# A graph layer on one core: 56 instead of 52 tiles fetched row by row, other waits for SyncE's transfers, and x gathered for 8 instead of 10 quads

## The chip, the cores and the metric

The kernel runs on one core of one Trainium2 chip. The metric is the device time of one execution in microseconds; the time before is the median of three runs. Engines are named as in the profile: PE (TensorE), PEld (its weight loads), DVE (VectorE), ACT (ScalarE), POOL (GpSimd) and SP (SyncE, which only issues transfers). A "q" behind an engine's name (ACTq, SPq) marks what its sequencer issues.

## The reference

A message-passing layer over 206,250 edges and 6,250 nodes of 128 features (8 heads of 16), with the edges sorted by receiver, followed by a residual and a normalization:

```python
w_ij = silu(edge_feats @ rad_W1 + rad_b1) @ rad_W2 + rad_b2
w_ij = w_ij + silu(chi_scalar @ sph_W1 + sph_b1) @ sph_W2 + sph_b2      # per edge, 128 wide
q_i = (x @ Wq)[receivers];  k_j = (x @ Wk)[senders];  v_j = (x @ Wv)[senders]
alpha = (q_i * w_ij * k_j).sum over each head / sqrt(16) * cutoffs
out = segment_sum(alpha * v_j, receivers) / 16
return layernorm(x + out)
```

## The kernel before, in words

**Tiles, quads, groups.** Edges are cut into tiles of 128; four tiles are a quad (512 edges), four quads a group. There are 403 quads in 101 groups. `order` is the order in which quads are worked on; the loop over `g` and `slot` handles one quad a slot, at place `i = 4 g + slot` of `order`.

**The start.** K and V of all nodes are computed in 13 chunks and stored to a table in device memory, `kv_tab` (L353), one row of 1 KB per node. Edges need the rows of their senders. The table isn't ready at once, so for the first `XQ` quads POOL gathers rows of x instead (`gather_x`, L134 writing `msg`), and PE projects them to K and V as it does the chunks. `AHEAD` is 14: the quads `order[XQ:14]` are gathered from `kv_tab` before the loop starts. Beside the start's quads PE transposes the receivers' relative places (`turn_rel`), which are stored as `rel_lin` and read back broadcast as `relb`, one transfer a group.

**Two ways to fetch rows.** The usual way is an indirect DMA of POOL (`gather`, L134), one per tile: 128 rows of `kv_tab`, so four a quad. For `ROW_TILES` quads, spread evenly over the places 20 to 392, the last tile is fetched otherwise: by 128 single transfers of one row (L191, into `wide`), 64 issued by SP and 64 by ACT, with the rows' addresses loaded into registers 32 at a time (L186). `load_rows(i)` runs at the end of every slot and issues the share of the tile that is due, so that the whole tile is on its way 8 places ahead of its quad. A quad with such a tile needs three gathers of POOL.

**A slot.** PE does sums of older messages (L614), the first layers of quad `i + 2` (L516, into `ph`), the receivers' q of quad `i + 1` (L525, into `pq`) and the second layers (L563, into `pw`). ACT applies the two activations of a quad (L546, `silus`), with copies of small products between them (`copies`), and later issues its row transfers. DVE multiplies `pq` by K (L575), by `pw` (L583), reduces over heads (L585), scales (L589) and forms messages with V (L602). POOL gathers for quad `i + 14`, each of the four gathers behind one of the last four `pw` products of an older quad (`old[-QT:]`).

**SP's transfers in the loop.** One each a group: x (L281), feats (L218), relb (L229) and the finished rows (`out`, L731). SP works its queue in order. x and feats carry a wait for a product of PE (`past`), so all that stands behind them in the queue waits too. Group sums are normalized four groups at a time; their rows are written by `write_rows(1, i)`.

Of the kernel before, what the change touches and what calls it, by code (L numbers as in the profile page):

```python
# [21 lines left out]
SP = mybir.EngineType.SP  # L22
ACT = mybir.EngineType.Activation
WAIT = mybir.DependencyInfo(mybir.DependencyClass.Sync, mybir.DependencyReason.DATA)

P = 128
# [9 lines left out]
NG = math.ceil(E / (P * GT))  # L36
NT = NG * GT
# [6 lines left out]
W = 32  # L44
LB = 4
ROW_BYTES = 2 * D * 4
XQ = 10
RING = 16
ROW_TILES = 52
ROW_FIRST = 20  # L50
ROW_LAST = 392
ROW_LEAD = 8
ROW_UNIT = 32
ROW_ACT = 64
XU = 4
WRITE_LAG = 3
READY_LAG = 2
# [3 lines left out]
XL = 3  # L61
# [6 lines left out]
def gnn_kernel(ctx, tc, x, src, dst, weight, edges, rad_W1, rad_b1, rad_W2, rad_b2,  # L68
# [38 lines left out]
    row = const.tile([P, 1], F32, name="row")  # L107
# [22 lines left out]
    def quad_of(name, bufs, width=D):  # L130
        return ep.tile([P, QT, width], F32, name=name, bufs=bufs)
# [11 lines left out]
    row_of = {}  # L143
    row_done = {}
    rows_left = {SP: [], ACT: []}
    row_sems = [tc.alloc_semaphore(f"rows_{n}") for n in range(ROW_SEMS)]
    row_count = [0] * ROW_SEMS

    def next_rows(engine, n):

        left = rows_left[engine]
        while n > 0 and left:
            row = next(left[0], None)
            if row is None:
                left.pop(0)
                continue
            row()
            n -= 1

    r_of = {}  # L160
    feats_of, relb_of, act_of, kv_of, hot_of, hotT_of, x_of, q_of, msg_of = ({} for _ in range(9))
# [11 lines left out]
    def load_rows(i):  # L173

        k = next((k for k in range(ROW_TILES) if i <= row_at[k] - ROW_LEAD), None)
        start = None if k is None else (row_at[k - 1] if k else ROW_FIRST) - ROW_LEAD + 1
        if k is None or i < start:
            return
        q = order[row_at[k]]
        slots = row_at[k] - ROW_LEAD + 1 - start  # L180
        table = kv_tab.bitcast(U8).rearrange("(o n) b -> o (n b)", o=1)

        def rows_by(engine, name, a, b):
            for e in range(a, b, ROW_UNIT):
                m = min(ROW_UNIT, b - e)
                rows = nc.values_load_multi_w_load_instructions(  # L186
                    at_i[k:k + 1, e:e + m], engines=(name,), min_val=0,
                    max_val=(N - 1) * ROW_BYTES,
                    skip_runtime_bounds_check_because="senders are nodes")[1]
                for p, r in zip(range(e, e + m), rows):  # L190
                    yield lambda p=p, r=r: signalled(engine.dma_start(  # L191
                        row_of[q][p:p + 1, 0, :].bitcast(U8), table[:, ds(r, ROW_BYTES)]))

        def signalled(o):
            tc.no_tile_sem_insts.add(o.ins.name)
            tc.add_to_no_dep_group(f"rows_{q}", o.ins)
            o.then_inc(row_sems[k % ROW_SEMS], 16)
            row_count[k % ROW_SEMS] += 16
            row_done[q] = row_sems[k % ROW_SEMS], row_count[k % ROW_SEMS]

        n = P - ROW_ACT
        if i == start:
            row_of[q] = quad_of("wide", 3, P)[:, :2, :].rearrange("p t d -> p (t d)")[:, None, :]
            rows_left[SP].append(rows_by(nc.sync, SP, 0, n))
            rows_left[ACT].append(rows_by(nc.scalar, ACT, n, P))
        for engine, m in ((SP, n), (ACT, ROW_ACT)):
            a, b = (math.ceil(m * j / slots) for j in (i - start, i - start + 1))
            next_rows(engine, b - a)

    def kv_parts(q, t):  # L210

# [4 lines left out]
    def load_feats(g, mark=None):  # L216
        feats_of[g] = gp.tile([P, EG // 2], F32, name="feats", bufs=3)
        o = nc.sync.dma_start(feats_of[g], edges[g])  # L218
        if mark is not None:
            tc.add_manual_dep(o.ins, mark.ins.name, WAIT, reason="one signal of TensorE a quad")  # L220
# [51 lines left out]
    def load_x(g, mark=None):  # L272

        if g not in r_of:
            n = min(XU, NG - g)
            rows = nc.values_load_multi_w_load_instructions(
                gb_i[:1, g:g + n], engines=(SP,), min_val=0, max_val=(N - P) * D * 4,
                skip_runtime_bounds_check_because="the table is clamped to it")[1]
            r_of.update(zip(range(g, g + n), rows))
        x_of[g] = gp.tile([P, D], F32, name="x", bufs=XL + 4)  # L280
        o = nc.sync.dma_start(x_of[g].bitcast(U8), rows_from(x, r_of[g]))  # L281
        if mark is not None:
            tc.add_manual_dep(o.ins, mark.ins.name, WAIT, reason="one signal of TensorE a quad")
# [21 lines left out]
    with tc.tile_pool(name="nodes", bufs=1) as nodes, \  # L305
# [21 lines left out]
                nc.sync.dma_start(xs[:N - (c + full) * P, full, :], x[(c + full) * P:, :])  # L327

        def gather_x(q):
            xs_of[q, "x"] = xs = quad_of("msg", XQ)  # L330
            for t in range(QT):
                gather(xs[:, t, :], x, src_x[:, q * QT + t:q * QT + t + 1])

# [100 lines left out]
        def turn_rel(t):  # L434

            n = min(P, NT - t)
            pt = nps.tile([P, QT, P], F32, name="pt", bufs=3)
            nc.tensor.transpose(pt[:n, 0, :], rel[:, t:t + n], ident)
            nc.scalar.activation(relT[:n, t // P, :], pt[:n, 0, :], AF.Copy)
# [38 lines left out]
        for i, (k, n) in enumerate(work):  # L478
            if i + 2 < len(work):
                turn(*work[i + 2])  # L480
            kvs = k_and_v(k, n)
            for o, w in smalls[i:i + 1]:
                nc.scalar.dma_start(o, w)
            if i >= len(chunks):
                kv_of[k[0]] = kvs
                a = (i - len(chunks)) * 5 // 4
                for t in range(a * P + P, min(((i - len(chunks) + 1) * 5 // 4 + 1) * P, NT), P):
                    turn_rel(t)
                for f in beside.get(i, []):
                    f()  # L490
                continue
            store(k, kvs)
            if k + 8 < len(chunks):
                load_nodes(k + 8)
            if k == 4:
                nc.sync.dma_start(src_i, src)
            for f in beside.get(k, []):
                f()
            if i == len(chunks) - 1:
                load_rel(0, gp, 1)  # L500
                load_feats(0)
                nc.sync.dma_start(scale, weight)
        for q in order[XQ:AHEAD]:
            gathers(q)
# [5 lines left out]
    with tc.tile_pool(name="ps", bufs=1, space=PSUM) as pp, tc.tile_pool(name="loop", bufs=1) as lp:  # L510
# [85 lines left out]
        def messages(q, alpha, t=slice(0, QT), marks=()):  # L596

            if t.start == 0:
                msg_of[q] = quad_of("msg", XQ)
            for u, kv in kv_parts(q, t):  # L600
                n = u.stop - u.start
                o = nc.vector.tensor_tensor(  # L602
                    msg_of[q][:, u, :].rearrange("p t (h e) -> p t h e", e=HD),
                    kv[:, :, D:].rearrange("p t (h e) -> p t h e", e=HD),
                    alpha[:, u.start - t.start:u.stop - t.start, :, None].to_broadcast(
                        [P, n, HEADS, HD]), op=OP.mult)
                behind(o, marks, 3)
# [39 lines left out]
        def part_sums(g):  # L647
            n = quads_in(g) * W
            part_of[g] = gp.tile([P, D], F32, name="part")
            nc.scalar.activation(part_of[g][:n, :], po_of[g][:n, :], AF.Copy)  # L650
# [103 lines left out]
            nc.vector.tensor_scalar(general, found, 0.0, None, op0=OP.is_gt)  # L754

        written, ready, ready_at = [], [], []
        load_feats(1)
        load_rel(1, lp, 4)
        load_feats(2)
        load_rel(2, lp, 4)  # L760
        for g in range(1, XL):
            load_x(g)
        silus(order[0], first_layers(order[0]))
        pick(1)
        q_at_edges(order[0])
# [1 line left out]
        multiply(order[0])  # L767
        marks = weigh(order[0])
        mark = marks[-1]
        for g in range(NG - 1):  # L770
            for slot, j in enumerate((0, 2, 1, 3)):
                q = g * NQ + j
                i = g * NQ + slot
                turned, past, old = None, mark, marks
                if slot == 0 and g == CHECK + len(checks) + 1:
                    verdict()
                if slot == 0:
# [7 lines left out]
                        mark = sum_quads(g - 1, t)  # L785
                first_layers(order[i + 2])
                mark = q_at_edges(order[i + 1])
                marks = weigh(order[i + 1])

                def copies():  # L790
                    if turned:
                        turned()
                    if 1 <= g and slot == 3:
                        part_sums(g - 1)

                silus(order[i + 2], mark, marks, copies)
                if ready and ready_at[-1] <= i:
# [5 lines left out]
                if slot == 0:  # L803
                    if g + XL < NG:
                        load_x(g + XL, past)
                if slot == 2:
                    if g + 3 < NG:
                        load_feats(g + 3, past)
                if slot == 3 and g + 3 < NG:
                    load_rel(g + 3, lp, 4)  # L810
                if slot == 0 and 1 <= g:
                    one_hots(g)
# [3 lines left out]
                        pick(g + 2)  # L816
                if slot == 2 and 1 <= g:
                    place(g - 1)
                write_rows(1, i)
                if slot == (3 if g < NG - 2 else 2):  # L820
                    if 2 <= g:
                        statistics(g - 2)
# [224 lines left out]
```

## Time and profile before

| what | value |
|---|---|
| median of three runs | 1974.61 us (1973.51 to 1975.46) |
| profiled execution | 1977.56 us |
| its span, first to last instruction | 1975.8 us |
| mean granted TensorE clock | 0.941 |
| PE, DVE, POOL, ACT busy | 90%, 77%, 75%, 33% |
| gathers of POOL | 40 of x, 1520 of kv |
| row transfers of SP, ACT | 3328 each |

A row of the timeline reads: start, duration, engine, line, operation, what is written and read, number of instructions merged, and in brackets the engine's idle time before it with what ended it. A row of a group ends with total and mean duration, then idle time before. Issuing a transfer does not count as busy time of ACT or SP.

### The profile page before, as it was taken

How to read it: one execution, taken by the hardware profiler on the slowest of the kernel's cores; microseconds unless marked ns; L12 is line 12 of the kernel's file. 1: busy time of each engine (PE TensorE's matmuls, PEld its weight loads, DVE VectorE, ACT ScalarE, POOL GpSimd, SP SyncE). 2: the span in 40 equal slices, each digit the busy share in tenths (PEclk: the TensorE clock that was granted, in tenths of full speed). 3: DMA queues.
4: the chain of work that ended last, by engine and by line, in shares of the span. 5: the costliest groups of instructions: out<-in, count | busy, mean ns of one | idle time of the engine just before them, and what ended most of it. 6: DMA issues, size and time to landing. Idle time of an engine off the chain costs nothing. (4 is left out here: it accounts for less than half of the span.)

```text
span 1975.8 us, 57697 instructions
## 1 busy us (share of the span) xinstructions
PE 1781.9 (90%) x16014; PEld 1482.9 (75%) x16014; DVE 1520.3 (77%) x3403; ACT 642.5 (33%) x1362; POOL 1481.0 (75%) x1570
## 2 busy tenths in 40 slices
PE   9799999999998999998989889988988888888998
PEld 8687778777777777777877777777767777777776
DVE  6688788888877777777777777776877877777778
ACT  3233333333233333332323332323323333232334
POOL 7777777777777777777777777777777777777775
PEclk9899999999989989899989999899999999898989
DMA  9455555555555555555555555555545455555543
GB/s 318 144 153 155 158 154 157 149 148 151 159 155 156 149 159 152 147 155 145 157 144 156 155 147 154 149 150 149 157 142 158 143 156 155 145 154 147 155 142 94
DMA packets 152293, 304.92 MB, mean 154 GB/s; under 512 B 39852, under 2 KB 86300, under 8 KB 151964
## 3 DMA queue, kind: packets, MB, share of 16 engines
q0 software_dynamic: 74240, 201.95, 36.4%
q1 hardware_dynamic: 69568, 95.42, 15.1%
q10 hardware_dynamic: 8156, 3.82, 0.9%
q8 instruction: 127, 2.08, 0.4%
q14 instruction: 202, 1.65, 0.3%
HBM read 287.58 MB, written 13.46 MB: 152 GB/s over the span
## 5 line engine op out<-in xcount | busy, mean ns | idle before, releaser
L134 POOL DMA_INDIRECT kv<-kv_tab,src_i x1520 | 1440.9, 948 | 469.1 <-PE pw L563 174.0
L546 ACT ACTIVATE act<-ph,b 128x512 f32<-128x512 f32 x806 | 554.8, 689 | 1275.2 <-PE pq L525 767.4
L563 PE MATMUL pw<-w,act 128*128 128x128 f32 x6448 | 883.1, 294 | 0.0
L563 PEld LDWEIGHTS pw<-w,act 128*128 128x128 f32 x6448 | 803.6, 203 | 96.7 <-issue 79.8
L516 PE MATMUL ph<-feats,w 32*128 32x512 f32 x1612 | 521.8, 670 | 38.3 <-ACT act L546 35.7
L525 PE MATMUL pq<-q,hotT 32*128 32x128 f32 x3224 | 489.3, 293 | 19.1 <-DVE kq L575 18.8
L575 DVE TENSOR_TENSOR kq<-pq,kv 128x512 f32<-128x512 f32 (+1 forms) x403 | 270.6, 671 | 285.4 <-DMA kv<-kv_tab,src_i 123.5
L525 PEld LDWEIGHTS pq<-q,hotT 32*128 32x128 f32 x3224 | 409.9, 195 | 49.8 <-DVE kq L575 47.9
L585 DVE TENSOR_REDUCE side<-kq 128x32 f32<-128x512 f32 x403 | 279.8, 694 | 42.7 <-PE pw L563 1.3
L602 DVE TENSOR_TENSOR msg<-kv,side 128x512 f32<-128x512 f32 (+1 forms) x404 | 270.3, 669 | 44.2 <-DVE side L589 2.4
L583 DVE TENSOR_TENSOR kq<-pw,kq 128x512 f32<-128x512 f32 x403 | 274.0, 680 | 0.0
L516 PEld LDWEIGHTS ph<-feats,w 32*128 32x128 f32 x1612 | 143.3, 190 | 144.4 <-ACT act L546 74.1
L558 PE MATMUL pw<-brow,onesb 3*128 3x512 bf16 x403 | 158.9, 394 | 0.6 <-DVE kq L583 0.6
L614 PE MATMUL po<-msg,hot 128*32 128x128 f32 x3200 | 156.8, 294 | 0.0
L655 PE MATMUL pq<-part,to 128*128 128x128 f32 x200 | 48.7, 328 | 88.8 <-DVE kq L575 88.5
L589 DVE TENSOR_TENSOR side<-side,scale 128x32 f32<-128x32 f32 x400 | 79.8, 200 | 42.6 <-DVE side L585 0.9
L655 PEld LDWEIGHTS pq<-part,to 128*128 128x128 f32 x200 | 32.9, 207 | 100.3 <-DVE kq L575 86.7
L614 PEld LDWEIGHTS po<-msg,hot 128*32 128x32 f32 x3200 | 72.3, 112 | 38.9 <-issue 5.6
L258 DVE TENSOR_TENSOR hotT<-relb,side 128x512 f32<-128x512 bf16 x101 | 68.7, 680 | 0.0
L252 PE MATMUL pq<-wq,xT 128*128 128x128 f32 x200 | 44.3, 305 | 26.5 <-DVE kq L575 26.1
L263 DVE TENSOR_TENSOR hot<-rel,side 128x512 f32<-128x512 f32 x100 | 68.0, 680 | 0.0
L252 PEld LDWEIGHTS pq<-wq,xT 128*128 128x128 f32 x200 | 32.4, 203 | 32.1 <-DVE kq L575 31.4
(121 smaller groups left out, 843.7 us busy)
## 6 DMA issues: line engine op xcount, KB each, us to landing
wide<-kv_tab SPq DMA_DIRECT2D x3328, 1.0 KB
wide<-kv_tab ACTq DMA_DIRECT2D x3328, 1.0 KB
feats<-in_edges SPq DMA_DIRECT2D x101, 512.0 KB
kv<-kv_tab,src_i POOLq DMA_INDIRECT x1520
relb<-rel_lin SPq DMA_DIRECT2D x101, 128.0 KB
x<-in_x SPq DMA_DIRECT2D x101, 64.0 KB
out<-y SPq DMA_DIRECT2D x101, 64.0 KB
kv_tab<-kv SPq DMA_DIRECT2D x12, 512.0 KB
```

The source lines that it names most:

```text
L134: return nc.gpsimd.indirect_dma_start(out=o, out_offset=None, in_=table, in_offset=bass.IndirectOffsetOnAxis(ap=index, axis=0))
L516: return nc.tensor.matmul(act_of[q, i], w1[r0:r0 + R, :], feats_of[g][r0:r0 + R, c0:c0 + EQ], start=True, stop=True)
L525: o = nc.tensor.matmul(pq_of[q][:, t, :], hotT_of[g][b, t * P:(t + 1) * P], q_of[g][b, :], start=True, stop=True)
L546: o = nc.scalar.activation(act, act_of[q, i], AF.Silu, bias=b1[:, i:i + 1])
L558: nc.tensor.matmul(pw, onesb, brow.rearrange("p t d -> p (t d)"), start=True, stop=False)
L563: o = nc.tensor.matmul(pw[:, t, :], act_of[q, i][:, t * P:(t + 1) * P], w2[:, i, :], start=False, stop=(t == QT - 1 and i == 1))
L575: o = nc.vector.tensor_tensor(kq_of[q][:, u, :], pq_of[q][:, u, :], kv[:, :, :D], op=OP.mult)
L583: nc.vector.tensor_tensor(m, pw_of[q][:, t, :], m, op=OP.mult)
L585: o = nc.vector.tensor_reduce(alpha, m.rearrange("p t (h e) -> p t h e", e=HD), AX.X, OP.add)
L602: o = nc.vector.tensor_tensor(msg_of[q][:, u, :].rearrange("p t (h e) -> p t h e", e=HD), kv[:, :, D:].rearrange("p t (h e) -> p t h e", e ...
L614: o = nc.tensor.matmul(po_of[g][j * W:(j + 1) * W, :], hot_of[g][:, j * QT + t, :], msg_of[g * NQ + j][:, t, :], start=(t == 0), stop=(t = ...
L655: nc.tensor.matmul(ph[:, :D], to[:n, 0, :], part[:n, :], start=True, stop=(g == 0))
```

## The change

Three things are changed together.

1. `ROW_TILES` goes from 52 to 56 over the same places, so four more quads have a tile of single rows. The rows due are kept in `owed`: SP's are all issued at the slot's end, ACT's but for two (`ROW_CARRY`), which are issued between the two activations of the next slot, one before and one after the small copy.
2. SP's loop transfers of x and feats wait for the product of PE one quad older (`seen[-2]` for `mark`); feats moves from slot 2 to slot 3 and relb from slot 3 to slot 2; `out` is written in slot 1 alone. At the start, x and feats of groups 1 and 2 are issued with the first group's, ahead of `scale`, where they stood behind the store of `rel_lin`.
3. `XQ` goes from 10 to 8: x is gathered and projected for 8 quads, and kv is gathered for `order[8:14]` ahead of the loop. `turn_rel` is spread over 8 quads; the message buffers stay 10 (`MSGS`).

```diff
-XQ = 10
+XQ = 8
+MSGS = 10
-ROW_TILES = 52
+ROW_TILES = 56
-ROW_UNIT = 32
+ROW_CARRY = 2
+ROW_UNITS = {SP: 32, ACT: 32}
@@ def next_rows(engine, n):
+    owed = {SP: 0, ACT: 0}
-        while n > 0 and left:
+        for _ in range(min(n, owed[engine])):
             row = next(left[0], None)
-            if row is None:
+            while row is None:
                 left.pop(0)
-                continue
+                row = next(left[0], None)
             row()
-            n -= 1
+            owed[engine] -= 1
@@ def load_rows(i):
-            return
+            return next_rows(ACT, owed[ACT])
...
             a, b = (math.ceil(m * j / slots) for j in (i - start, i - start + 1))
-            next_rows(engine, b - a)
+            owed[engine] += b - a
+        next_rows(SP, owed[SP])
+        next_rows(ACT, owed[ACT] - ROW_CARRY)
@@ the start
-                a = (i - len(chunks)) * 5 // 4
-                for t in range(a * P + P, min(((i - len(chunks) + 1) * 5 // 4 + 1) * P, NT), P):
-                    turn_rel(t)
+                a, b = ((j - len(chunks)) * (math.ceil(NT / P) - 1) // XQ for j in (i, i + 1))
+                for t in range(a + 1, b + 1):
+                    turn_rel(t * P)
...
                 load_feats(0)
+                for g in range(1, XL):
+                    load_x(g)
+                    load_feats(g)
                 nc.sync.dma_start(scale, weight)
...
-        load_feats(1)
         load_rel(1, lp, 4)
-        load_feats(2)
         load_rel(2, lp, 4)
-        for g in range(1, XL):
-            load_x(g)
@@ the loop
+        seen = [mark] * 3
-                turned, past, old = None, mark, marks
+                turned, past, old = None, seen[-2], marks
                 mark = q_at_edges(order[i + 1])
+                seen.append(mark)
                 def copies():
+                    next_rows(ACT, 1)
                     if turned:
                         turned()
                     if 1 <= g and slot == 3:
                         part_sums(g - 1)
+                    next_rows(ACT, 1)
-                if slot == 2:
-                    if g + 3 < NG:
-                        load_feats(g + 3, past)
                 if slot == 3 and g + 3 < NG:
+                    load_feats(g + 3, past)
+                if slot == 2 and g + 3 < NG:
                     load_rel(g + 3, lp, 4)
-                write_rows(1, i)
+                if slot == 1:
+                    write_rows(1, i)
```

More of the change, by code (lines that the diff above doesn't have):

```diff
@@ L183, in rows_by @@
         def rows_by(engine, name, a, b):
-            for e in range(a, b, ROW_UNIT):
-                m = min(ROW_UNIT, b - e)
+            for e in range(a, b, ROW_UNITS[name]):
+                m = min(ROW_UNITS[name], b - e)
                 rows = nc.values_load_multi_w_load_instructions(
@@ L329, in gather_x @@
         def gather_x(q):
-            xs_of[q, "x"] = xs = quad_of("msg", XQ)
+            xs_of[q, "x"] = xs = quad_of("msg", MSGS)
             for t in range(QT):
@@ L598, in messages @@
             if t.start == 0:
-                msg_of[q] = quad_of("msg", XQ)
+                msg_of[q] = quad_of("msg", MSGS)
             for u, kv in kv_parts(q, t):
```

## The prediction

> **What bounds the kernel now.** I read the page's busy shares first, then its costliest groups, then the timeline of GpSimd (POOL), then who waited for whom, then the consumer's pace by stretches.
>
> ```profile
> PE 1781.9 (90%) x16014; PEld 1482.9 (75%) x16014; DVE 1520.3 (77%) x3403; ACT 642.5 (33%) x1362; POOL 1481.0 (75%) x1570
> L134 POOL DMA_INDIRECT kv<-kv_tab,src_i x1520 | 1440.9, 948 | 469.1 <-PE pw L563 174.0
> L134 POOL DMA_INDIRECT msg<-in_x,src_x x40 | 38.2, 954 | 13.2 <-issue 11.9 <-DMA src_x<-in_src 1.3
> ```
>
> By the shares TensorE (PE, 90%) looks like the bound and POOL (75%) does not. The second row corrects this: POOL was idle for 469.1 us before its 1520 gathers, 0.31 us each, and the timeline shows the same 0.30 before nearly every gather, whoever is named as releaser. It belongs to the gather: one costs 0.95 + 0.30 = 1.25 us of POOL, busy or not.
>
> ```profile
> 2.95 1.10 POOL L134 DMA_INDIRECT msg<-in_x,src_x  x1 [1.34 <-DMA src_x<-in_src]
> ...
> 43.33 0.94 POOL L134 DMA_INDIRECT msg<-in_x,src_x  x1 [0.30 <-issue]
> ...
> 53.32 0.94 POOL L134 DMA_INDIRECT kv<-kv_tab,src_i  x1 [0.30 <-DVE b_left L380]
> ...
> 82.31 0.95 POOL L134 DMA_INDIRECT kv<-kv_tab,src_i  x1 [3.88 <-PE pw L563]
> ...
> 1962.06 0.95 POOL L134 DMA_INDIRECT kv<-kv_tab,src_i  x1 [0.31 <-PE po L614]
> ```
>
> These are the first gather of x, the 33rd, the first gather of kv, the 21st (four quads ahead of the loop and one in its first slot make 20 before it) and the last (1520th). From the 21st to the last there are 1499 steps in 1962.06 - 82.31 = 1879.75 us, 1.254 us each: POOL issues without a pause from 82.31 to 1963.0. The only large hole is the one before 82.31, 3.88 - 0.30 = 3.58 us.
>
> Does the rest of the kernel keep up with it? The products' reduction (L585) runs once a quad, so its count in a stretch is the consumer's pace.
>
> ```profile
> core 0: us, DVE busy (x), PEclk, DMA share, GB/s
> 112.00:462.00 350.00, 55.54 (x80) 0.97 0.53 152
> 500.00:1900.00 1400.00, 201.35 (x290) 0.94 0.53 152
> DVE kq L575 <- DMA kv<-kv_tab,src_i: 123.5, 85, 3.5
> ```
>
> While gathered quads are in stock, one takes 350/80 = 4.375 us; from 500 us on, when the stock is gone, 1400/290 = 4.83 us. POOL's own pace is (4 - 52/372) x 1.254 = 4.84 us a quad (a row tile, one every 372/52 quads, spares one gather of four). So for three quarters of the run VectorE waits for gathers (123.5 us in 85 waits), and the end is set by POOL's list of 1560 gathers. The profiled execution took 1977.56 us, its span 1975.8; the median of the three runs is 1974.61. I make the sum on the profiled execution and move the median by the same amount.
>
> **The change, part by part.** *Fewer gathers.* ROW_TILES 52 to 56 takes one kv gather from each of four quads; XQ 10 to 8 takes 8 gathers of x away and adds 8 of kv (two quads more are gathered). So 1520 + 8 - 4 = 1524 of kv and 32 of x, 1556 in all, 4 fewer. In terms of the list: the first kv gather moves from 53.32 to where the 33rd gather stands now, 43.33: -9.99 us; four kv gathers more: 4 x 1.254 = +5.02. Together -4.97 us, all on the path.
>
> *Is the table ready at 43.33?* The gathers read kv_tab, whose last store must have landed.
>
> ```profile
> L353 SPq DMA_DIRECT2D kv_tab<-kv x13: 332/343/353, 9.8 to 37.3; - x13
> 38.39 0.45 SPq L218 DMA_DIRECT2D feats<-in_edges  x1
> 38.88 0.44 SPq L502 DMA_DIRECT2D scale<-in_weight  x1
> 44.00:46.00 2.00, 1.39 (x3) 1.00 0.79 294
> 46.00:48.00 2.00, 1.70 (x2) 1.00 0.33 87
> ```
>
> The last store is issued at 37.3; behind it in the same queue stand relb (128 KB), feats (512 KB) and scale (808 KB). The DMA engines fall from 79% to 33% busy at about 46.5, so all of it is through by then. 1.45 MB at the 294 GB/s of the first window is some 4.9 us, which puts the table's landing near 41.6 (an estimate). That is 1.7 us before it is needed. Bounds: 0, or, if the table were only complete at 48, 48 - 43.3 = 4.7 us. I take 0. The transfers that the change puts ahead of scale (two feats, two x) are queued behind the stores and cannot delay them.
>
> *The hole before 82.31.* That gather waits for the second quad's pw products. Those were late because PE stood waiting for x of group 1:
>
> ```profile
> 68.77 2.46 SPq L281 DMA_DIRECT2D x<-in_x  x3
> 76.41 0.77 PE L243 MATMUL pq<-pick,x 128*128 128x128 f32 x2 [7.11 <-DMA x<-in_x]
> 79.53 3.26 PE L563 MATMUL pw<-w,act 128*128 128x128 f32 x16
> 48.14 0.60 PE L337 MATMUL pt<-ident,msg 128*128 128x128 f32 x4
> 50.42 0.60 PE L337 MATMUL pt<-ident,msg 128*128 128x128 f32 x4
> ```
>
> After the change these loads of x and feats stand with the first quad's, before scale, so the 7.11 us go; and two quads fewer are projected at the start, 50.42 - 48.14 = 2.28 us each. The second quad's products then end at about 79.53 + 3.26 - 7.1 - 4.6 = 71.1. POOL gets to that gather (now the 29th of kv) at 43.33 + 28 x 1.254 = 78.4. The margin is 7 us, so the hole goes: -3.58 us. What is late next there: relb of group 1, which still waits for the store of rel_lin; it is read two quads into the loop and lies under the same margin. The rest of the start's gain (some 8 us of PE) only lengthens the stock, since POOL has the end.
>
> *Four more row tiles: 512 more transfers of 1 KB,* half on SyncE's queue (SP), half on ScalarE's (ACT).
>
> ```profile
> 1007.33 0.69 ACT L546 ACTIVATE act<-ph,b 128x512 f32<-128x512 f32 x1 [4.89 <-PE pw L563]
> 1007.52 0.55 ACTq L191 DMA_DIRECT2D wide<-kv_tab  x2
> 1007.92 0.27 ACT L650 ACTIVATE part<-po 128x128 f32<-128x128 f32 x1
> 1008.07 0.69 ACT L546 ACTIVATE act<-ph,b 128x512 f32<-128x512 f32 x1
> 1008.16 2.13 ACTq L191 DMA_DIRECT2D wide<-kv_tab  x7
> L186 ACTq TENSOR_LOAD <-at_i x104: 2130/2204/2500, 128.9 to 1869.6; - x104
> L186 SPq TENSOR_LOAD <-at_i x104: 1866/2177/2488, 120.3 to 1862.8; - x104
> 1006.06 5.80 SPq L191 DMA_DIRECT2D wide<-kv_tab  x18
> ```
>
> Seven issues in 2.13 us, the last 0.23 long: (2.13 - 0.23)/6 = 0.317 us each, and a load of 32 addresses 2.20 us, two a tile. On ACT that is 64 x 0.317 + 2 x 2.20 = 24.7 us a tile, now every 372/52 = 7.15 quads (3.45 us a quad), then every 6.64 (3.72): +0.27 us a quad. The worst it can do is to lengthen the consumer's free pace by all of it, 4.375 + 0.27 = 4.64, still below POOL's new pace of (4 - 56/372) x 1.254 = 4.83. So it is covered, by 0.19 us a quad; without this cover it would cost 372 x 0.27 = 100 us. The lower end is 0. On SP it is (5.80 - 0.23)/17 = 0.328 us an issue and 2.18 us a load, 25.4 us a tile: 3.54, then 3.82 us a quad.
>
> *Two of ACT's issues between a quad's activations.* The rows above show that the sequencer already issues rows while the first activation runs (two at 1007.52, before the copy starts at 1007.92). Two issues take 0.63 us and lie under an activation of 0.69 us: nothing, at most 0.1 us in a chain that has slack.
>
> *SP's waits.* x and feats wait for products one quad older, feats and relb change slots, out is issued in slot 1 only, one a group, which is the rate at which groups are finished.
>
> ```profile
> SPq L218 <- PE pq L525: 100.7, 27, 12.7
> SPq L218 <- PE pw L563: 73.1, 45, 7.9
> SPq L281 <- PE pq L525: 52.8, 27, 6.2
> SPq L731 <- DMA out<-y: 54.0, 33, 6.7
> L281 SPq DMA_DIRECT2D x<-in_x x101: 327/355/1383, 25.1 to 1894.4; - x101
> L731 SPq DMA_DIRECT2D out<-y x100: 332/379/904, 138.3 to 1969.5; - x100
> ```
>
> 226.6 us of waiting for products go or shrink; the 54.0 of out's writes may stay. What queues behind such a wait on SP are row transfers, relb and out; all are needed several quads later (rows are issued at least 7 quads ahead). Gain on the path: 0; it is the room in which SP's extra 0.28 us a quad fits.
>
> *The end.* From the last gather's end (1963.0) to the span's end are 12.8 us of products, sums and the last write; nothing in them is changed.
>
> **Sum.** -4.97 - 3.58 = -8.55 us. Profiled execution 1969.0, span 1967.2, last gather's end near 1954.4; median 1974.61 - 8.55 = 1966.0 us.
>
> [...] A gather holds POOL for 1.25 us while the 16 DMA engines are 53% busy: issue is the scarce thing here, not transfer. [...]
>
> **The rivals.**
> [...]
> (2) *The start gives it back*: the table lands late (up to 4.7 us) and a wait of PE on relb reopens the hole (3.58): 1966.0 + 4.7 + 3.6 = 1974.3, no change. With the table alone late, 1970.7.
> (3) *Slower: SP becomes the bound.* Its work is 3.82 us of rows a quad, plus x, feats, relb and out once a group, some 0.4 us each by the rows above, 0.40 a quad: 4.22. If its waits do not shrink (226.6 + 54.0 us over 403 quads, 0.70), it needs 4.92 against POOL's 4.83, rows come late and VectorE waits for them. It decides from 4.83 on; at 4.92 the end is 372 x 0.09 = 33 us later than my forecast, 1999. Before, the same sum was 3.54 + 0.40 + 0.70 = 4.64 against 4.84. Against: these waits are there because SP is early; an SP that is late finds the products done.
>
> **How the numbers follow.** Forecast 0.72, rival 1 0.05, rival 2 0.13 (half of it the late table alone), rival 3 0.10. The range: down to 1962, if the two short pauses of POOL that I left in (1.5 us) and 2.5 us at the end go too; up to 1973, which takes in rival 1, the late table and 2 us of scatter at the end. Left out: rival 3 and the far half of rival 2. A measurement of this kernel tells about 0.2% (4 us) from no change, so "faster" is below 1970.7: forecast, nearly all of the late table and half of rival 1, 0.80; same 0.11; slower 0.09.
>
> **What the profile after would show.** Right: 1556 gathers, kv from about 43.3, no hole near 78 to 82, 1.25 us steps to about 1954.4, VectorE still waiting for kv from some point on (later than 500 us, since ACT and SP have more to issue), 12.8 us after the last gather. Wrong: a gap before the first kv gather (table), holes in POOL's list where it waits for products (consumer too slow), VectorE waiting for row transfers, or waits for DMA kv gone altogether with PE or ACT in their place.

## The result and the profile after

The changed kernel takes 1991.86 us (median of 4, 1990.48 to 1992.73) where the kernel before took 1975.03 (4 runs beside it, 1973.51 to 1976.06). The ratio is 1.0085, with a 95% interval of 1.0068 to 1.0103: slower by 17 us. The forecast was 1966.0 us. The profiled execution took 1990.48 us, its span 1988.4.

The page of the changed kernel, the busy shares and the group of the gathers:

```profile
PE 1788.7 (90%) x15990; PEld 1494.6 (75%) x15990; DVE 1521.5 (77%) x3411; ACT 647.0 (33%) x1360; POOL 1474.3 (74%) x1566
L136 POOL DMA_INDIRECT kv<-kv_tab,src_i x1524 | 1441.8, 946 | 489.2 <-PE pw L571 185.0
```

The count is the forecast one, 1524 gathers at the same 0.95 us. But the idle time before them grew from 469.1 to 489.2 us, although the hole of 3.58 us had been expected to go. The timeline of POOL shows where:

```profile
43.26 0.95 POOL L136 DMA_INDIRECT kv<-kv_tab,src_i  x1 [0.30 <-DVE kv L353]
...
77.53 0.94 POOL L136 DMA_INDIRECT kv<-kv_tab,src_i  x1 [0.30 <-issue]
78.78 0.95 POOL L136 DMA_INDIRECT kv<-kv_tab,src_i  x1 [0.30 <-PE pw L571]
80.03 0.95 POOL L136 DMA_INDIRECT kv<-kv_tab,src_i  x1 [0.30 <-PE pw L571]
...
265.12 0.95 POOL L136 DMA_INDIRECT kv<-kv_tab,src_i  x1 [0.30 <-PE pw L571]
267.21 0.94 POOL L136 DMA_INDIRECT kv<-kv_tab,src_i  x1 [1.14 <-PE pw L571]
...
278.48 0.95 POOL L136 DMA_INDIRECT kv<-kv_tab,src_i  x1 [0.30 <-PE pw L571]
282.71 0.95 POOL L136 DMA_INDIRECT kv<-kv_tab,src_i  x1 [3.28 <-DVE to L653]
...
1973.00 0.94 POOL L136 DMA_INDIRECT kv<-kv_tab,src_i  x1 [0.30 <-issue]
```

The start is as forecast: first gather of kv at 43.26, no hole near 78. Then there are pauses such as those before 267.21 and 282.71. Summed over all gaps above 0.36 us, each less the usual 0.30, they come to 24.25 us (before, from 100 us on: 1.54), 15.6 us of it between 230 and 460 us. The releasers named there change from pause to pause, and DVE's tile `to`, named for the longest, is nothing that a gather waits for: the real one has to be found elsewhere. How many gathers POOL issued in three stretches, before and then after:

```profile
core 0: us, POOL busy (x), PEclk, DMA share, GB/s
112.00:232.00 120.00, 90.69 (x97) 0.96 0.53 154
232.00:462.00 230.00, 172.86 (x183) 0.98 0.53 151
462.00:1900.00 1438.00, 1087.59 (x1148) 0.94 0.53 152
```

```profile
core 0: us, POOL busy (x), PEclk, DMA share, GB/s
112.00:232.00 120.00, 90.70 (x97) 0.99 0.52 153
232.00:462.00 230.00, 162.03 (x172) 0.93 0.50 146
462.00:1900.00 1438.00, 1080.79 (x1143) 0.93 0.52 151
```

11 gathers are missing in the second stretch and 5 in the third: 16 x 1.254 = 20 us. That is the miss. (The pauses grew by 22.7 us; without them a step is 1.251 us instead of 1.253, which gives 3 us back over 1523 steps.) The DMA engines are no busier on average (0.50 and 0.52), and the clock is not the cause: the stretch in which POOL lost most stands at 0.93, the same as the third, and an experiment below with 1146 gathers in the third stretch had 0.92 there.

**What POOL waits for.** In the trace each gather signals one of eight semaphores in turn, with never more than 16 increments recorded, and before a semaphore is used again POOL waits on it. Most gathers that come after a pause start 0.76 to 0.79 us after the last increment of the gather eight before (20 of 28, below): gather n waits for the last part of gather n - 8. At POOL's pace gather n starts 8 x 1.25 - 0.95 = 9.05 us after that gather's end, and a gather that waits starts 0.76 us after the increment, so the last part has some 8.3 us to land. From the times of the increments (14.4 to 15.9 of 16 are recorded), the mean us from a gather's end to its last increment but one ("15th") and to its last ("16th"), in three stretches; the same for five experiments told below. "Row" is the mean time from ScalarE's issue of a single row to the start of that row's packet. "Pauses" are POOL's from 100 us on; "lead" is how long before a gather POOL's sequencer has passed its wait (median):

```
                        80-110 us    250-400 us        500-1850 us      pauses  lead
                        15th  16th   15th  16th  row   15th  16th  row
before                  2.20  2.53   2.23  6.05  4.50  2.18  3.97  2.47   1.54  4.82
after                   1.93  2.07   2.12  7.67  6.46  2.13  5.90  4.40  24.25  2.83
after, 52 tiles         1.98  2.13   2.20  6.99  5.68  2.13  3.23  1.85   7.08  5.59
after, SP's old order   2.16  2.32   2.09  6.28  4.79  2.18  5.17  3.63   6.76  3.73
after, old waits        2.04  2.18   2.08  7.23  6.43  2.15  5.82  4.29  26.26  2.95
after, out's old place  2.05  2.28   2.16  6.63  5.33  2.18  4.98  3.45   8.29  3.90
after, feats' old place 2.31  2.46   2.13  7.60  6.45  2.15  5.52  4.11  16.84  3.09
```

Fifteen parts of a gather land some 2.2 us after its end on average, in both kernels never later than 4.8. So does the sixteenth until the row transfers begin (the first at 110 us); from then on it alone is late, between 250 and 400 us by 3.8 us before and by 5.6 after the change. In the changed kernel 34% of the gathers between 250 and 400 us pass the 8.3 us, before none. Of the 28 gaps above 0.5 us, 20 end 0.76 to 0.79 us after such a late increment (12.4 us of pauses). The other 8 end 3.34 to 3.40 us after it (10.6 us): about every 133 us POOL's sequencer stands still for 3.10 us, in both kernels; a lead of 4.8 us hides that but for two pauses, a lead of 2.8 does not.

That is what it would look like if one DMA engine of the 16 carried the single rows and fell behind: theory R of the expectations below. It is my inference: the trace has no numbers of engines, and no run shows which engines a row or a part of a gather takes. One late increment in sixteen agrees with it.

The packets of the rows agree too. ScalarE's rows are the only packets of 1 KB in their queue, one a row (3584), and only 9 of them overlap another in time (with every second one shifted by 0.14 to 0.52 us, 252 to 615 would). A row's packet starts 0.85 us after its issue at the earliest; the "row" columns show that most rows wait several us. This lag goes with that of the gathers: in each of the seven runs of the table, the delay of a gather's last part and the lag of the row that starts just before it have a correlation of 0.86 to 0.91. (SyncE's rows share their queue with relb's packets of the same size and can't be told apart.)

**What SyncE waited for.** The waits of the changed kernel:

```profile
DVE kq L583 <- DMA kv<-kv_tab,src_i: 147.6, 102, 3.6
SPq L223 <- PE pq L533: 95.6, 28, 10.1
SPq L223 <- PE pw L571: 35.3, 45, 7.9
SPq L739 <- DMA out<-y: 12.6, 7, 2.8
PEld ph L524 <- ACT act L554: 94.9, 141, 2.2
```

VectorE still waits for gathers, more than before (123.5). The waits for products are still there: the three rows whose sum was 226.6 us now make 167.4. The small row is the one that matters: SyncE's waits between writes of out fell from 54.0 us to 12.6. The timeline of SyncE before, and then after:

```profile
1029.45 0.38 SPq L731 DMA_DIRECT2D out<-y  x1
1029.93 2.85 SPq L191 DMA_DIRECT2D wide<-kv_tab  x9
1033.97 0.38 SPq L731 DMA_DIRECT2D out<-y  x1
1034.45 5.14 SPq L191 DMA_DIRECT2D wide<-kv_tab  x9
...
1040.22 0.38 SPq L731 DMA_DIRECT2D out<-y  x1
...
1044.34 0.40 SPq L731 DMA_DIRECT2D out<-y  x1
```

```profile
1001.33 0.39 SPq L739 DMA_DIRECT2D out<-y  x1
...
1020.22 0.39 SPq L739 DMA_DIRECT2D out<-y  x1
```

Four groups are finished together. Before, they are written in four slots in a row, and each write waits for the one before it to have landed. That too hangs on one late part: before, the last increment but one of a write of out comes 2.4 us after its issue and the last 4.1; with out's old place put back into the changed kernel (below) 2.3 and 5.6. After, one is written per group, the one before 18.9 us earlier, and of the wait 12.6 us are left.

### The profile page after: what moved, and what is told of

Same layout as the page of the kernel before. It is cut to its first block, busy times and chain, and to the rows that moved or that the text cites. A ratio compares the mean times of both kernels' runs of the same rounds, so it can differ in the third digit from the quotient of the medians.

```text
span 1988.4 us, 58734 instructions
## 1 busy us (share of the span) xinstructions
PE 1788.7 (90%) x15990; PEld 1494.6 (75%) x15990; DVE 1521.5 (77%) x3411; ACT 647.0 (33%) x1360; POOL 1474.3 (74%) x1566
## 5 line engine op out<-in xcount | busy, mean ns | idle before, releaser
L136 POOL DMA_INDIRECT kv<-kv_tab,src_i x1524 | 1441.8, 946 | 489.2 <-PE pw L571 185.0
L524 PE MATMUL ph<-feats,w 32*128 32x512 f32 x1612 | 544.0, 680 | 47.5 <-ACT act L554 46.1
L533 PE MATMUL pq<-q,hotT 32*128 32x128 f32 x3224 | 495.1, 295 | 8.7 <-DVE kq L583 8.6
L533 PEld LDWEIGHTS pq<-q,hotT 32*128 32x128 f32 x3224 | 414.9, 197 | 29.5 <-DVE kq L583 28.1
L524 PEld LDWEIGHTS ph<-feats,w 32*128 32x128 f32 x1612 | 150.5, 192 | 161.5 <-ACT act L554 94.9
L663 PE MATMUL pq<-part,to 128*128 128x128 f32 x200 | 49.1, 331 | 107.4 <-DVE kq L583 106.9
L257 PE MATMUL pq<-wq,xT 128*128 128x128 f32 x200 | 43.0, 299 | 18.9 <-DVE kq L583 18.6
```

The costliest lines, as they stand in the source:

```text
L136: return nc.gpsimd.indirect_dma_start(out=o, out_offset=None, in_=table, in_offset=bass.IndirectOffsetOnAxis(ap=index, axis=0))
L524: return nc.tensor.matmul(act_of[q, i], w1[r0:r0 + R, :], feats_of[g][r0:r0 + R, c0:c0 + EQ], start=True, stop=True)
L533: o = nc.tensor.matmul(pq_of[q][:, t, :], hotT_of[g][b, t * P:(t + 1) * P], q_of[g][b, :], start=True, stop=True)
L663: nc.tensor.matmul(ph[:, :D], to[:n, 0, :], part[:n, :], start=True, stop=(g == 0))
```

## The experiments

In three of the seven sessions of experiments the kernel before took 1974 to 1975 us. In the other four the granted clock was about 0.82 and it took 2619 to 2653 us; those runs, last below, are read apart. Each ratio is against the kernel before in the same session.

**52 row tiles in the changed kernel.**

```diff
-ROW_TILES = 56
+ROW_TILES = 52
```

> The changed kernel with 52 row tiles again, once more, because the first run of it was on a chip where the kernel before takes 2624 us and POOL waits for TensorE throughout, so that POOL's list was not the bound there. Where the kernel before takes about 1975 us: theory R (all single-row transfers share one DMA engine, whose part of each gather lands late and holds the gather eight places on) expects 1971 to 1980 us and pauses of POOL under 10 us; rival S (SyncE's order and shorter waits make the loss) and rival C (ScalarE's issues between activations make it) expect 1985 to 1995 us.

1978.58 us, ratio 1.0019 (1.0010 to 1.0028). POOL's windows:

```profile
232.00:462.00 230.00, 168.95 (x179) 0.96 0.53 152
462.00:1900.00 1438.00, 1087.32 (x1150) 0.94 0.52 151
```

Seven of the eleven missing gathers are back and all of the later ones. Pauses 7.08 us, in the range expected. The count of rows is a condition of the loss; but even so this kernel, whose list starts 10 us earlier, has eight gathers of kv more and no hole, is no faster than before. The kernel before with 56 tiles was run at the lower clock only (below), so the count alone, with SyncE's old order, has no time here at the full clock.

**SyncE's old order and waits, all of it, with 56 tiles.**

```diff
-                turned, past, old = None, seen[-2], marks
+                turned, past, old = None, mark, marks
...
-                if slot == 3 and g + 3 < NG:
-                    load_feats(g + 3, past)
-                if slot == 2 and g + 3 < NG:
+                if slot == 2:
+                    if g + 3 < NG:
+                        load_feats(g + 3, past)
+                if slot == 3 and g + 3 < NG:
                     load_rel(g + 3, lp, 4)
...
-                if slot == 1:
-                    write_rows(1, i)
+                write_rows(1, i)
```

> The changed kernel with SyncE's old order and waits, 56 tiles, where the kernel before takes about 1975 us: theory R by the count of rows alone 1985 to 1992 us; rival S 1966 us; both together between.

1971.05 us, ratio 0.9981 (0.9972 to 0.9990): faster than both kernels. SyncE's order is the other condition. ScalarE's two issues between activations are still in this kernel, so they are not what made the loss. Its waits, and VectorE's:

```profile
SPq L739 <- DMA out<-y: 130.9, 59, 7.8
DVE kq L583 <- DMA wide<-kv_tab: 74.5, 19, 6.2
DVE kq L583 <- DMA kv<-kv_tab,src_i: 23.3, 10, 4.4
```

SyncE is held 130.9 us at out, so rows come late and VectorE waits 74.5 us for them, as my rival 3 said. It costs nothing: POOL's list goes on meanwhile (183 gathers between 232 and 462 us, as before), and VectorE waits for gathers less.

**Rows in pieces.** The row described as 2, and as 16, pieces in both access patterns.

```diff
-row_of[q][p:p + 1, 0, :].bitcast(U8), table[:, ds(r, ROW_BYTES)]
+row_of[q][p:p + 1, 0, :].bitcast(U8).rearrange("p (a b) -> p a b", a=2),
+table[:, ds(r, ROW_BYTES)].rearrange("p (a b) -> p a b", a=2)
```

> The changed kernel, each row transfer described as 2 pieces of 512 bytes instead of 1 of 1024. Theory R: if the pieces go to two DMA engines, the first one moves half the bytes of the rows; the last part of a gather lands sooner (5 to 6 us after its issue instead of 7.7 where quads are in stock), POOL pauses less than the 24 us of the changed kernel, 1966 to 1985 us where the kernel before takes 1975. If the pieces stay on one engine there are only more packets on it: as slow as the changed kernel or slower, 1990 to 2010. Rivals S and C: 1992 us, no effect, since the issues are the same in number and place.

> The same with 16 pieces of 64 bytes. Theory R: no engine lags behind the others any more (the last part of a gather lands within 0.5 us of the one before it), POOL's pauses are gone, and the time is the forecast, 1966 us, where the kernel before takes 1975; unless 16 packets a row load all engines so far (16 x 19 packets a quad, 0.05 us each or more, beside the gathers) that all of them lag: then slower than 1992. Rivals S and C: 1992 us, or more if SyncE and ScalarE take longer to issue 16 pieces.

1991.63 us (1.0078, 1.0064 to 1.0092) and 1992.16 us (1.0082, 1.0068 to 1.0096). These two edits changed nothing that shows: an issue of a row takes 228 ns in the median in both, as in the changed kernel, and the pages of the changed kernel and of the run with 2 pieces have the same packets but for one, so the two pieces did not become packets of their own.

```profile
DMA packets 153261, 305.51 MB, mean 154 GB/s; under 512 B 40300, under 2 KB 87260, under 8 KB 152924
```

```profile
DMA packets 153262, 305.51 MB, mean 153 GB/s; under 512 B 40301, under 2 KB 87261, under 8 KB 152925
```

They serve as two repeats of the changed kernel (25.9 and 27.4 us of pauses).

**SyncE's old waits alone** (the first hunk of the old order).

> The changed kernel with SyncE's old waits alone, for a chip where the kernel before takes about 1975 us. Waits as the cause of POOL's pauses: 1968 to 1976 us, pauses near 7 us. Places as the cause: 1986 to 1994 us, pauses over 20 us. Each a part: between.

1990.36 us, ratio 1.0076 (1.0063 to 1.0090), pauses 26.26 us. Which product x and feats wait for is not the cause.

```profile
SPq L739 <- DMA out<-y: 14.0, 8, 2.6
```

**Out's old place alone** (the last hunk), and **feats' and relb's alone** (the middle one).

> The changed kernel with out's old place alone: a finished group may be written in any slot, not in slot 1 only. With the whole old order SyncE waited 130.9 us in 59 waits for earlier writes of out before the next one (12.6 us in 7 waits in the changed kernel). If that wait is what held SyncE's rows back whenever the row engine was behind, it comes back here (over 80 us), the pauses of POOL fall to 5 to 10 us, and VectorE waits for rows instead: 1968 to 1976 us where the kernel before takes about 1975. If feats' and relb's places are the cause: 1986 to 1994 us with over 20 us of pauses.

> The changed kernel with feats in slot 2 and relb in slot 3 again, out in slot 1 only. If out's place is the cause: 1986 to 1994 us, pauses over 20 us, and few waits of SyncE for out (under 30 us). If these two places are: 1968 to 1976 us. If both places give a part, both runs lie between.

Out in any slot: 1974.29 us, ratio 0.9997 (0.9988 to 1.0006), 17.6 us less than the changed kernel. Its waits and windows:

```profile
SPq L739 <- DMA out<-y: 129.6, 60, 8.9
DVE kq L583 <- DMA wide<-kv_tab: 52.2, 14, 7.4
```

```profile
232.00:462.00 230.00, 170.29 (x180) 0.95 0.52 147
462.00:1900.00 1438.00, 1084.95 (x1147) 0.92 0.53 152
```

Feats and relb exchanged again: 1986.76 us, ratio 1.0064 (1.0050 to 1.0078), 5 us less.

```profile
SPq L739 <- DMA out<-y: 15.0, 8, 3.6
```

So of the 21 us that SyncE's order costs with 56 tiles, out's place makes 17 and the places of feats and relb some 5. The wait comes back with out's place, ScalarE's rows wait 1.1 and 0.95 us less for their packets in the two stretches, the last part of a gather lands 1.0 and 0.9 us earlier, and the pauses fall from 24 to 8 us.

**Sessions at the lower clock.** The same kernels with 52 tiles, 56 tiles in the kernel before, the new start alone (x for 8 quads, early loads, in the kernel before), and parts of SyncE's old order:

> The changed kernel with 52 row tiles again; its start, SyncE's order and waits and the issues between activations stay. Theory R (every single-row transfer runs on one and the same DMA engine; with 56 tiles that engine's share of a gather lands up to 10 us late, and the gather eight places on, which waits for it, pauses): with 7% fewer rows the last part of a gather lands about 6 us after its issue as in the kernel before, POOL's pauses fall from 24 us to under 10, and the time is the forecast plus four gathers, 1966 + 5 = 1971 us, up to 1980 if SyncE's denser issue keeps part of the lag. Rival S (SyncE's order and shorter waits alone make the lag, by letting rows and feats out in a rush): about 1988 to 1995. Rival C (ScalarE's issues between activations delay TensorE): about 1985 to 1992.

> The kernel before with 56 instead of 52 row tiles and nothing else. Theory R: the last part of a gather lands later than the 6 us of the kernel before, POOL's pauses grow from 5 us by 5 to 20 us, and what four gathers less save (5 us) is lost: 1975 to 1990 us. Rivals S and C: nothing that they name is in it, so 1975 - 5 = 1970 us.

> The kernel before with the new start alone: x gathered for 8 quads, x and feats of groups 1 and 2 loaded ahead of scale; 52 tiles, SyncE's old order. All theories that put the loss into the loop (R, S, C): the hole of 3.58 us goes, the first kv gather moves 9.99 us forward and eight more follow at 1.254 us, 1975.0 - 3.58 - 9.99 + 10.03 = 1971.5 us. If the start itself carries part of the loss (a larger stock in hand lets the loop run longer at its fast pace, with rows packed closer, so that the lag of theory R begins): 1975 to 1982 us.

> The changed kernel with SyncE's old order: x and feats wait for the newest products, feats in slot 2, relb in slot 3, out in every slot. 56 tiles, the new start and the issues between activations stay. Theory R with the count of rows alone: still slow, 1985 to 1992 us, last parts of gathers 7 us late and more. Rival S: 1966 us, POOL's pauses under 5 us. Both together: between, 1972 to 1984.

> The changed kernel with SyncE's old waits alone (x and feats again wait for the newest products); feats, relb and out stay where the change put them. If the waits are what spaces the transfers (SyncE, held once or twice a group, sends its rows later and less densely, and the lag of the row engine stays under the 9 us at which POOL must wait): as with the whole old order, 1968 to 1975 us, pauses of POOL near 7 us. If the places are the cause (feats right behind relb and ahead of a full slot of rows): still 1986 to 1994 us with pauses over 20.

> The complement: feats, relb and out in their old slots, but x and feats wait for products one quad older, as in the changed kernel. If the waits are the cause: 1986 to 1994 us, pauses over 20 us. If the places are: 1968 to 1975. If each gives a part: both this and the run with the old waits lie between, 1976 to 1986.

> The kernel before with the new start alone, where the kernel before takes about 1975 us and POOL's list is the bound: the hole of 3.58 us goes, the first kv gather moves 9.99 us forward, eight gathers more follow at 1.254 us: 1971.5 us, with pauses of POOL under 5 us. If a larger stock makes the loop run ahead so far that the lag of the row engine reaches POOL: 1973 to 1980.

> The kernel before with 56 row tiles and nothing else, where the kernel before takes about 1975 us. Theory R with both causes needed: as in the run with SyncE's old order, the row engine lags 0.2 to 1 us more than before, pauses grow from 5 to at most 9 us, and the four gathers less give 5 us: 1970 to 1976 us. If the count of rows alone were enough to stop POOL (pauses of 15 us and more): 1980 to 1990 us.

With 52 tiles: changed kernel 1.0012 (0.9997 to 1.0026), start alone 0.9999 (0.9981 to 1.0016) and again 0.9994 (0.9980 to 1.0008). With 56: kernel before 1.0121 (1.0090 to 1.0153) and again 1.0155 (1.0132 to 1.0177), SyncE's old order 1.0119 (1.0091 to 1.0147), old places 1.0153 (1.0132 to 1.0175), old waits 1.0209, 1.0146 and 1.0170 in three sessions (the last two were run on the same expectation). POOL's list does not bind there; it waits for TensorE's products, as the waits of the changed kernel with 52 tiles show (262 of them, up to 21.9 us long):

```profile
POOL kv L136 <- PE pw L571: 467.0, 262, 21.9
```

Only some 4 of 16 increments of a gather are recorded in these traces, so they don't show whether its last part is late. But ScalarE's rows start 1.1 to 1.4 us after their issue (in the table 1.9 to 6.5), so there is hardly a backlog of rows, and these runs say nothing on the cause above. They show something else: at that clock four tiles more cost 1.2 to 2.1% in every order tried, and the start gains nothing. What makes those four tiles cost 32 to 54 us there was not settled. VectorE waits 30 to 55 us for rows in the four runs with out's old place, but not in the three with out in slot 1 alone, which lose as much.

**Rows as two halves with a space between** (also at the lower clock), so that they stay two packets.

```diff
-row_of[q][p:p + 1, 0, :].bitcast(U8), table[:, ds(r, ROW_BYTES)]
+row_of[q][p:p + 1, ::2, :].bitcast(U8),
+table[:, ds(r, ROW_BYTES)].rearrange("p (a b) -> p a b", a=2)
```

> The changed kernel, in which each row of keys and values lands as two halves of 512 bytes with a space between them in SBUF (products and messages read the halves there), so that the two pieces can no longer be joined into one packet as they were in the two runs with rows in pieces. The issues keep their number, place and waits. Theory R (the one engine of the rows lags): with the halves on two engines its load of row bytes halves, the last part of a gather lands 2 us or more earlier than in the changed kernel where quads are in stock (7.7 us there), the pauses fall under 10 us, and the time is 1966 to 1976 us. If both halves go to the same engine, or if each packet costs the engine the same whatever its size: pauses as before or more, 1992 or slower. A cause in SyncE's or ScalarE's sequencers: 1992 with the last part early.

4039.97 us, ratio 1.52 (1.518 to 1.526). Its issues of rows, min, median and max in ns:

```profile
L194 SPq DMA_DIRECT2D wide<-kv_tab x3584: 2/562/2150, 196.5 to 3972.2; - x200
L194 ACTq DMA_DIRECT2D wide<-kv_tab x3584: 2/570/1404, 217.5 to 3950.0; - x200
```

In the changed kernel the medians are 228 ns on both. A second piece makes the issue 2.5 times as long, on two queues that had little room; whether that alone makes 4040 us was not settled. (The pieces do go apart: 167,597 packets, 14,336 more than in the changed kernel, which is two for each of 7168 rows.) That says nothing on theory R, since POOL's list was far from the bound. Rows in more pieces at no cost in issue were not found, so the lag itself was never removed with 56 tiles and everything else unchanged.

## Why the prediction was wrong

- *The bound, the gathers' count, the table, the hole*: right. POOL's list sets the end; first kv gather forecast at 43.33, found at 43.26; the 29th forecast at 78.4, found at 78.78 without a hole. With SyncE's old order these gains show in part: 1971.05 us against 1974.35 in the same session, 3.3 of the 8.55 us forecast, with 5.2 us of pauses more than before.
- *"512 more transfers of 1 KB ... so it is covered"*: this step failed. I costed the rows on the queues that issue them and on the consumer's pace, and at nothing on the engines that move them, because the 16 together were 53% busy. The term was 0 us; measured, the pauses of POOL are 24.25 us (1.54 of them were there before), and the list ends at 1973.95 instead of 1954.4.
- *"Gain on the path: 0" for SyncE's waits*: this failed too, and on the other side of zero. I listed the 54.0 us at out as something that "may stay" and asked what is queued behind it (rows, needed late). I did not ask what the wait holds back: with it gone, ScalarE's rows wait 6.46 and 4.40 us for their packets in the two stretches, with out's old place 5.33 and 3.45. Its price is 17 us with 56 tiles. The 226.6 us of waits for products, which I thought the point of the edit, did not go (167.4 are left) and matter little: with the old waits the kernel stays at 1990 us.
- *Two issues between activations*: TensorE's weight loads wait more for ScalarE's activations (94.9 us, before 74.1), off the path as assumed; with 52 tiles that wait is 49.1 us. It was not tried alone; with SyncE's old order it is 108.7 us and the kernel takes 1971 us.
- *The end*: 12.8 us forecast, 14.4 measured; the 1.6 us were not explained.
- *The sum*: list +19.6, end +1.6, together 21.2 us of span (1967.2 to 1988.4). The other 4.7 us between 1966.0 and 1991.86 are mostly scatter between a profiled execution and the median (1977.56 against 1974.61 before, 1990.48 against 1991.86 after).
- *The rivals*: the first, given 0.05, was that the DMA engines set the pace of the gathers, so that tiles moved off POOL bring nothing and only the hole goes (1974.61 - 3.58 = 1971.0 us, part of the range). No run shows that: POOL's steps before are 1.25 us at a DMA share of 0.79 (44 to 46 us) as at 0.53, and in the changed kernel the gathers that do not wait keep that step at 0.50 to 0.52. What came late was one part in sixteen, which a mean over the engines does not show. The third (SyncE the bound, rows late) did not happen in the changed kernel, and where it did, in the two kernels with out's old place, it cost nothing. The sign that I gave for "wrong", holes in POOL's list, was right; that they would be waits for products was not.

That the sixteenth part is late only while rows run, that most pauses end right behind it, that both the rows' number and SyncE's hold at out move it, and that the rows' own packets lag with it, is shown. That the rows of both queues and the late part lie on one and the same engine is inferred from this; no record names an engine.

## What to carry to other kernels

The mean share of sixteen DMA engines, 0.52 to 0.53, did not show here that one part in 16 of a gather came late: look at when the last two increments of a gather land, before and after small transfers begin (in the kernel before 2.20 and 2.53 us after its end between 80 and 110 us, 2.23 and 6.05 between 250 and 400). Before a wait is taken off a queue, ask which backlog it keeps short, not only who stands behind it (out's wait: 17 us). A list that seems gapless may lean on a lead: here a median lead of 4.82 us went with 1.54 us of pauses, one of 2.83 us with 24.25.

## What the runs showed of the hardware

- A gather that reuses one of eight semaphores waits for the last of the increments, at most 16, of the gather eight before: in the changed kernel 20 of 28 pauses above 0.5 us end 0.76 to 0.79 us after it. At 1.25 us a gather that leaves some 8.3 us.
- While 7168 rows of 1 KB are fetched one by one, one part in 16 of a gather lands 3.8 us after the others on average (5.90 us against 2.13 from the gather's end, changed kernel, 500 to 1850 us), with the DMA engines 52% busy.
- POOL's sequencer stands still for 3.10 us about every 133 us in the traces of both kernels; with a median lead of 4.8 us two of these pauses showed, with 2.8 us eight.
- A row transfer of 1 KB in one piece takes 228 ns to issue in the median in the changed kernel, and 227 and 228 with SyncE's old order at the lower clock; in two pieces with a space between them 562 and 570.
- In the sessions with a granted clock of about 0.82 the kernel before takes 33% more (2619 to 2653 us against 1975), with TensorE instead of POOL at the bound. The clock alone does not make that (a product of pw lasts 330 ns instead of 295), and the rest was not explained. Edits rank differently there: SyncE's old order is 0.9981 at the full clock and 1.0119 there.
